# Biases by matmul, halves written across partitions, and a first convolution in half columns

## The chip, the cores and the metric

The kernel runs on one core of one Trainium2 chip. The core has five engines that work beside each other and wait for each other through semaphores: PE (TensorE: matrix products; its weight loads are listed apart as PEld), DVE (VectorE), ACT (ScalarE), POOL (GpSimd) and SP (SyncE, which here only issues DMA transfers). Data lie in SBUF, whose 128 partitions are the rows of every tile; PE writes its results to PSUM, from where ACT and DVE take them. The metric is the device time of one execution in microseconds (us), lower is better.

## What is computed

Four images of 128 channels and 64 by 64 = 4096 positions go through two layers. Layer 0 normalises the image, makes three 1x1 convolutions with a PReLU, and mixes the positions by a softmax over 4096 by 4096 scores. Layer 1 normalises each position's 128 channels, applies an attention with 16 heads of 8 channels whose queries, keys and values are all the same tensor, a feed-forward part, and at last a recurrence over the positions. The reference, cut to what matters here:

```python
def _L0_conv_ref(x, w1, b1, a1, w2, b2, a2, wa, ba, aa):
    e1 = _conv1x1(x, w1, b1, a1).reshape(N, -1, HW)      # 64 channels
    e2 = _conv1x1(x, w2, b2, a2).reshape(N, -1, HW)      # 64 channels
    asm = _conv1x1(x, wa, ba, aa).reshape(N, C, HW)      # 128 channels
    score = jnp.einsum('nci,ncj->nij', e1, e2)
    score = jax.nn.softmax(score, axis=2)
    out = jnp.einsum('nij,ncj->nci', score, asm)

def _L1_attn_ref(x, ...):
    qkv = _qz_ring(heads + rx_theta)
    attn = softmax(einsum('bhsd,bhtd->bhst', q, q) / np.sqrt(D))
    ctx = einsum('bhst,bhtd->bhsd', attn, q)
    attn_out = ctx @ w_comb.T + b_comb
    x1 = _ln(x + attn_out, g1, beta1)
    zf = jnp.cos(x1[..., :NQ_FFN]) * jnp.cos(ry_theta)
    h = jax.nn.relu(zf @ w1.T + b1)
    ffn_out = h @ w2.T + b2
    return _ln(x1 + ffn_out, g2, beta2)

def step(yt, wx_t):                                       # over all positions
    yt = jax.nn.sigmoid(wx_t + yt @ Vt)
```

## The kernel before

**Stages.** For each image n from 0 to 3 there is a convolution stage (`first_stage`, layer 0) and an attention stage (`second_stage`). The feed-forwards of image n run inside the convolution stage of image n+1, eight of them (one for 512 positions each), cut into small steps that are interleaved with that stage's own work; those of image 3 run alone in a `third_stage`. Then the recurrence runs and the output is written. In each stage the order of the instructions on PE, ACT and DVE (in attention on POOL too) is the order in which the code issues them, so an instruction that waits holds up all that stand behind it on its engine.

**Two float32 formats.** A float32 matmul is made of two passes over its columns. A float32r matmul is one pass and rounds its operands; where the kernel needs more precision it splits a number in a high part (rounded) and a low part (the rest) and stacks the two along the partitions, or makes two matmuls.

**The start of a convolution stage** (`layer0`). The image `xs` is normalised in eight pieces of 512 columns (`normalised`, L364, DVE). `both_convs(i)` convolves 1024 columns with w1 and w2 at once (L379, PE; result in PSUM pair `pc`), ACT makes the two halves of the PReLU (`y` L324, `z` L325), DVE joins them (L326) into `e1`, whose partitions 0 to 63 hold the first convolution and 64 to 127 the second. Then DVE writes the rounded second convolution to partitions 64 to 127 of `e2` (L386) and the rest to a scratch (L388), and two DMAs on SP's queue move 64 partitions each: `e1` low to `e1` high (L389), the scratch to `e2` low (L390). So `e2` has high and low parts of the second convolution stacked, and `e1` twice the first. `halves(ic)` splits 512 columns of `e1` into high and low parts (L425, L426) as the moving operand `hl`. `scores(ic, jp)` multiplies `e2` with both parts of `hl` (L442, two matmuls for each 128 rows), ACT takes the exponential (L446), DVE sums (L451, L454). `weigh` multiplies with `asmT` (L461), `take` copies the sum out (L473). `third_conv(i)` makes `asmT`: a matmul of ones with `ba_rows` writes the bias first (L396), then L405 adds the product; a PReLU follows. The order at the start is: pieces 0 and 1 normalised, `both_convs(0)` (the other six pieces within it, ahead of its L326), `halves(0)`, `third_conv(0)`, `both_convs(1)`, then the scores, with the other convolutions between them (list `pieces`, one popped at a time).

**Attention.** 8 head pairs by 4 query blocks. A block is a row of turns (20 in the first two blocks, 16 in the others); a turn makes scores for two key tiles and both heads (L956), exponentials (ACT, L968), and two turns later the product with the values (`weigh`, L807). Since scores are symmetric, a tile off the diagonal is used a second time, transposed: DVE transposes (L773), and after four turns of a group 16 `mirror_step`s (L786, eight small matmuls each) multiply into one of two halves of PSUM `misc`, and DVE adds that to `later` (L800), which frees the half. `finish` transposes the block's result (L841). How many mirror steps follow a turn is set by a credit: each turn adds a rate and each step takes one.

```python
rates = (3.3, 3.0) if b < NQB // 2 else (3.15, 3.0)
credit = min(credit + rates[0 if off else 1], 4.0)
```

A turn that is not `off` has its tiles on the diagonal; `end_of_all` is the last block of the last head pair. In that last block the statistics of the next image (L337 to L352) are issued too. What is left of the mirror steps after the last turn is done at the start of the next stage, around the first L364 and L379.

**A feed-forward** (`feed_forward`). POOL adds `bc_bc` (b_comb in every partition) to `x1` (L1075). PE transposes `q`, ACT copies it (`cT`, L1078), PE multiplies with `wc_sb` (L1083) and DVE adds `x1`, giving `v` (L1085). `v` is normalised (statistics on DVE, the power on POOL at L241, ACT at L283), DVE multiplies g1 (L1092), and POOL adds `fb2_bc` (which holds fb2 + beta1) into `x1` (L1093). A cosine of eight channels follows, then two matmul layers (L1129, ACT relu L1138, L1148 into `po`); L1158 adds `x1`, and two more normalisations and a residual (L1165, L1168) follow. In `third_stage` the last pieces of attention (`left`: L823 to L882) are done first, by DVE, POOL and ACT in turn.

**Setup.** Small weights are loaded on POOL's queue, then ACT's. `cos_steps` on `ry_sb` and a product with `f1_all` make `f_low`, part of which a DMA on SP (L311) moves to `f1_sb`.

Of the kernel before, what the change touches and what calls it, by code (L numbers as in the profile page):

```python
# [26 lines left out]
def kernel(  # L27
# [136 lines left out]
    ba_rows = const.tile([P, P], F32, tag="ba_rows", name="ba_rows")  # L164
    nc.gpsimd.memset(ba_rows, 0.0)
# [20 lines left out]
    wc_sb, bc_bc = load(w_combT, "wc_sb"), load_row(b_comb, "bc_bc")  # L186
# [9 lines left out]
    ba_all = setup_pool.tile([33, P], F32, tag="ba_all", name="ba_all")  # L196
    nc.gpsimd.memset(f1_all, 0.0)
    for i in range(2):
        nc.scalar.dma_start(out=ba_all[ds(32 * i, 1), :], in_=ba)
# [3 lines left out]
    fb1_sb, f2_sb, fb2_bc = load(fb1, "fb1_sb"), load(f2T, "f2_sb"), load_row(fb2, "fb2_bc")  # L203
# [8 lines left out]
    nc.vector.tensor_tensor(fb2_bc, fb2_bc, be1_bc, ALU.add)  # L212
# [80 lines left out]

    def blocks(ap):
        return ap.rearrange("p (k e) -> p k e", e=P)
# [8 lines left out]
    for _ in cos_steps(cry, ry_sb, ck, cr):  # L304
# [8 lines left out]
    nc.vector.tensor_copy(ba_rows[0:1, :].bitcast(F32R), ba_all[0:1, :])  # L313
    nc.vector.tensor_copy(ba_rows[32:33, :].bitcast(F32R), ba_all[32:33, :])
    nc.vector.tensor_tensor(
        ba_rows[32:33, :].bitcast(F32R), ba_all[32:33, :], ba_rows[32:33, :], ALU.subtract
# [38 lines left out]
    def layer0(n, xs, xh, norm, shifted, begin, meanwhile):  # L355
# [12 lines left out]
        e1, e2 = get("e", f"e1_{n}"), get("e", f"e2_{n}")  # L368
# [4 lines left out]

        def both_convs(i):

            cols = ts(i, 2 * IC)
            pc = pair_psum(f"pc{n}_{i}")
            for j in range(2):
                nc.tensor.matmul(  # L379
                    pc[:, j, :], w12_sb, xh[:, ts(2 * i + j, IC)], start=True, stop=True  # L380
                )
            y, z = mid_tile(f"y{n}_{i}"), mid_tile(f"z{n}_{i}")
            if i == 0:
                normalised(2, NIC)
            prelu(pair(e1[:, cols]), pc, y, z, (b12_sb, minus_b12), a12_sb)
            nc.vector.tensor_copy(pair(e2[CR:P, cols]).bitcast(F32R), pair(e1[CR:P, cols]))  # L386
            low = y[CR:P]
            nc.vector.tensor_tensor(low, pair(e1[CR:P, cols]), pair(e2[CR:P, cols]), ALU.subtract)  # L388
            nc.sync.dma_start(out=e1[CR:P, cols], in_=e1[0:CR, cols])  # L389
            nc.sync.dma_start(out=pair(e2[0:CR, cols]), in_=low)  # L390

        def third_conv(i):

            pc = pair_psum(f"pa{n}_{i}")
            for j in range(2):
                nc.tensor.matmul(  # L396
                    pc[:, j, :],
# [80 lines left out]
        if not shifted:  # L478
            halves(0)
# [1167 lines left out]
```

## Time and profile before

| what | us |
|---|---|
| three executions | 7203.8, 7194.3, 7195.15 (median 7195.15) |
| profiled execution, device time | 7196.66 |
| its span in the trace | 7194.9 |
| convolution stages (24 to 415, 1660 to 2165, 3420 to 3920, 5180 to 5690) | 391, 505, 500, 510 |
| attention stages (415 to 1660, 2165 to 3420, 3920 to 5180, 5690 to 6945) | 1245, 1255, 1260, 1255 |
| last feed-forwards (6945 to 7075) | 130 |
| recurrence and end (7075 to 7195) | 120 |

The stage borders are rounded to 5 us from the timeline; the convolution stage of image 0 is shorter since it has no feed-forwards in it. The engines over the span, from the first part of the page:

```profile
PE 6875.7 (96%) x92974; PEld 3726.6 (52%) x92974; DVE 5958.0 (83%) x8037; ACT 5994.8 (83%) x11903; POOL 2783.9 (39%) x9957
```

Each entry is an engine, its busy time, the share of the span, and its instructions. The costliest groups of the whole span (line, engine, operation, tiles and shapes, count; busy time and mean of one in ns; idle time of the engine just before, and what ended most of it):

```profile
L968 ACT ACTIVATE e<-s 128x1024 f32<-128x1024 f32 (+1 forms) x3480 | 2947.9, 888 | 89.6 <-PE s L956 40.7
L773 DVE STREAM_TRANSPOSE t<-e 128x1024 f32<-128x1024 f32 x2240 | 2586.2, 1209 | 10.1 <-ACT e L968 7.5
...
L786 PE MATMUL misc<-t,mirror 128*32 128x128 f32 x57344 | 1994.0, 273 | 28.4 <-DVE later L800 25.6
```

All three belong to attention. Busy time of PE overlaps from one matmul to the next, so it is read against the length of a stage, not summed.

### The profile page before, as it was taken

How to read it: one execution, taken by the hardware profiler on the slowest of the kernel's cores; microseconds unless marked ns; L12 is line 12 of the kernel's file. 1: busy time of each engine (PE TensorE's matmuls, PEld its weight loads, DVE VectorE, ACT ScalarE, POOL GpSimd, SP SyncE). 2: the span in 40 equal slices, each digit the busy share in tenths (PEclk: the TensorE clock that was granted, in tenths of full speed). 3: DMA queues.
4: the chain of work that ended last, by engine and by line, in shares of the span. 5: the costliest groups of instructions: out<-in, count | busy, mean ns of one | idle time of the engine just before them, and what ended most of it. 6: DMA issues, size and time to landing. Idle time of an engine off the chain costs nothing. (4 is left out here: it accounts for less than half of the span.)

```text
span 7194.9 us, 224876 instructions
## 1 busy us (share of the span) xinstructions
PE 6875.7 (96%) x92974; PEld 3726.6 (52%) x92974; DVE 5958.0 (83%) x8037; ACT 5994.8 (83%) x11903; POOL 2783.9 (39%) x9957
## 2 busy tenths in 40 slices
PE   8999999998989999999898999999999999999977
PEld 4545555555554555554555455555455555555546
DVE  6678899887778999889676998888877788898884
ACT  3479999995558999999455999999855699999976
POOL 0024444434223454443423354444432244444541
PEclk9999999999999999999999999999999999999988
DMA  1010000001111000000011100000001100000012
GB/s 39 30 40 26 29 20 22 21 8 38 39 40 44 25 21 20 21 23 21 29 40 43 37 22 21 21 24 22 23 30 39 45 33 21 22 26 27 11 59 108
DMA packets 85394, 221.20 MB, mean 31 GB/s; under 512 B 9490, under 2 KB 10644, under 8 KB 83588
## 3 DMA queue, kind: packets, MB, share of 16 engines
q1 hardware_dynamic: 79904, 195.10, 8.1%
q8 instruction: 731, 11.98, 0.7%
q10 hardware_dynamic: 4164, 11.41, 0.4%
q14 instruction: 307, 2.51, 0.1%
q0 software_dynamic: 288, 0.20, 0.0%
HBM read 141.63 MB, written 56.62 MB: 28 GB/s over the span
## 5 line engine op out<-in xcount | busy, mean ns | idle before, releaser
L968 ACT ACTIVATE e<-s 128x1024 f32<-128x1024 f32 (+1 forms) x3480 | 2947.9, 888 | 89.6 <-PE s L956 40.7
L773 DVE STREAM_TRANSPOSE t<-e 128x1024 f32<-128x1024 f32 x2240 | 2586.2, 1209 | 10.1 <-ACT e L968 7.5
L786 PEld LDWEIGHTS misc<-t,mirror 128*32 128x32 f32 x57344 | 1664.5, 110 | 1409.0 <-issue 1350.7
L786 PE MATMUL misc<-t,mirror 128*32 128x128 f32 x57344 | 1994.0, 273 | 28.4 <-DVE later L800 25.6
L968 ACT ACTIVATE xs<-s 128x1024 f32<-128x1024 f32 (+1 forms) x2152 | 1835.0, 893 | 33.7 <-PE s L956 19.9
L773 DVE STREAM_TRANSPOSE t<-xs 128x1024 f32<-128x1024 f32 x1344 | 1558.8, 1209 | 2.2 <-ACT xs L968 0.8
L807 PE MATMUL acc<-e,q_aug 128*32 128x512 f32 x11360 | 1524.5, 609 | 0.0
L956 PE MATMUL s<-queries,keys 32*128 32x512 f32 x9216 | 1228.6, 497 | 23.1 <-ACT e L968 16.7
L849 POOL COPY own<-o 32x36 f32<-32x36 f32 x2048 | 432.3, 211 | 1730.8 <-DVE o L841 1650.9
L461 PE MATMUL acc<-p,asmT 128*128 128x512 f32 x2048 | 960.9, 602 | 2.5 <-ACT taken L473 2.5
L807 PE MATMUL acc<-xs,q_aug 128*32 128x512 f32 x7072 | 942.2, 605 | 0.0
L446 ACT ACTIVATE p<-s 128x1024 f32<-128x1024 f32 x512 | 499.9, 1022 | 458.3 <-PE s L442 457.3
L454 DVE TENSOR_TENSOR total<-total,p 128x1024 f32<-128x1024 f32 x448 | 564.7, 1260 | 278.0 <-ACT p L446 255.0
L956 PEld LDWEIGHTS s<-queries,keys 32*128 32x128 f32 x9216 | 483.6, 182 | 517.7 <-issue 368.5
L874 POOL COPY other<-turned 32x64 f32<-32x64 f32 x1904 | 445.8, 234 | 640.6 <-DVE turned L864 562.1
L743 POOL COPY mirror<-q 32x128 f32<-32x128 f32 x2048 | 596.8, 291 | 239.3 <-PE misc L786 151.4
L968 ACT ACTIVATION_READ_ACCUMULATOR e<-s 128x1 f32 x2880 | 649.0, 225 | 0.0
L442 PE MATMUL s<-hl,e 128*128 128x512 f32 x2048 | 608.7, 440 | 29.5 <-DVE hl L426 22.8
L461 PEld LDWEIGHTS acc<-p,asmT 128*128 128x128 f32 x2048 | 383.2, 192 | 338.9 <-issue 314.0
L442 PEld LDWEIGHTS s<-hl,e 128*128 128x128 f32 x2048 | 393.2, 196 | 184.4 <-issue 98.9
L800 DVE TENSOR_TENSOR later<-later,misc 128x128 f32<-128x128 f32 (+1 forms) x576 | 162.6, 282 | 375.8 <-PE misc L786 372.6
L834 POOL COPY by_token<-by_key 32x4 f32<-32x4 f32 x2016 | 388.6, 193 | 85.1
(258 smaller groups left out, 4788.1 us busy)
## 6 DMA issues: line engine op xcount, KB each, us to landing
keys<-parts_dram SPq DMA_DIRECT2D x256, 256.0 KB
queries<-parts_dram SPq DMA_DIRECT2D x1024, 32.0 KB
fx<-x_dram SPq DMA_DIRECT2D x64, 256.0 KB
x_dram<-x SPq DMA_DIRECT2D x56, 256.0 KB
xs<-in_x_dram SPq DMA_DIRECT2D x16, 512.0 KB
t_dram<-t2T SPq DMA_DIRECT2D x32, 256.0 KB
t2s<-t_dram SPq DMA_DIRECT2D x16, 512.0 KB
parts_dram<-high SPq DMA_DIRECT2D x28, 256.0 KB
```

The source lines that it names most:

```text
L442: nc.tensor.matmul(s[:, j, :], stationary, moving, start=y == 0, stop=y == len(parts) - 1)
L446: nc.scalar.activation(p, s, AF.Exp)
L454: nc.vector.tensor_tensor(state[ic], state[ic], p, ALU.add)
L461: nc.tensor.matmul(state["acc", ic], asmT[:, ts(2 * jp + j, P)], p[:, j, :], start=jp == 0 and j == 0, stop=jp == NP - 1 and j == 1,)
L743: nc.gpsimd.tensor_copy(wv[ts(a, 32), s, :, :, ts(a, D)], own[ts(s, 32)])
L773: nc.vector.transpose(group["e"][h][:, k, :], es[h])
L786: nc.tensor.matmul(state["acc"][ts(2 * x + h, 32), :], state["w"][:, QT * (s // 4) + TG * x + s % 4, h, :], state["e"][h][:, :, ds(IC * x ...
L807: nc.tensor.matmul(it["in"]["acc"][ts(2 * h + x, 32), :], it["qa"][:, ds((2 * it["tiles"][x] + h) * V, 32)], it["e"][h][:, ts(x, IC)], sta ...
L849: nc.gpsimd.tensor_copy(own[ts(s, 32), ts(x, 4), h, :], ov[ts(2 * h + x, 32), s, :, 0:V])
L874: copy(to[ts(k, 32), h], tv[ts(2 * x + h, 32), k])
L956: nc.tensor.matmul(ss[h][:, x, :], keys[unit[x] // QT].bitcast(F32R)[r, ts(unit[x] % QT, P)], queries[b].bitcast(F32R)[r, :], start=True, ...
L968: nc.scalar.activation(es[h][:, ts(x, IC)] if split else es[h], ss[h][:, x, :] if split else ss[h].rearrange("p x c -> p (x c)"), AF.Exp, ...
```

## The change

1. *Biases of the feed-forward.* One tile `bias_rows` holds ba, b_comb and fb2 + beta1 as high part in partition 0 and low part in partition 32, zeros elsewhere. `bias_first` multiplies ones with one of the three and starts the accumulation; it serves the third convolution as before, and now also L1083 and L1148. The two POOL additions, and the tiles `bc_bc` and `fb2_bc`, go; `v` takes `x1`'s place, and `fhalf` has one buffer less.
2. *Parts of e.* One tile `e12` holds both convolutions; DVE writes the rounded second convolution to `e2` high, and the low part straight to `e2`'s partitions 0 to 63 (inputs in partitions 64 to 127). The DMAs L389 and L390 go. `halves` works on 64 partitions; its result is copied to the other 64 by a DMA on SP, or, for the first columns of each image, by two ACT copies.
3. *First pieces.* The first convolution's PReLU and joins go by half columns (512); the six later pieces are normalised in two lots behind the first joins; `third_conv(0)` uses two single PSUM tiles; `both_convs(1)` moves behind the first two scores, as the first of the popped pieces.
4. *Credit.* The cap goes from 4.0 to 4.75, and diagonal turns of the last block have a rate of 4.5. Mirror steps that follow the five turns of a group in the first two blocks become 4, 4, 3, 3, 2 (before 4, 3, 3, 3, 3); a group in the other blocks ends one turn earlier.

The diff, cut to its core:

```diff
-    ba_rows = const.tile([P, P], F32, tag="ba_rows", name="ba_rows")
+    bias_rows = const.tile([P, 3, P], F32, tag="bias_rows", name="bias_rows")
...
     for i in range(2):
-        nc.scalar.dma_start(out=ba_all[ds(32 * i, 1), :], in_=ba)
+        for k, ap in enumerate((ba, b_comb, fb2, be1)):
+            nc.scalar.dma_start(out=biases[ds(32 * i, 1), k, :], in_=ap)
...
-    nc.vector.tensor_copy(ba_rows[0:1, :].bitcast(F32R), ba_all[0:1, :])
-    nc.vector.tensor_copy(ba_rows[32:33, :].bitcast(F32R), ba_all[32:33, :])
+    for row in (0, 32):
+        at = slice(row, row + 1)
+        nc.vector.tensor_tensor(biases[at, 2], biases[at, 2], biases[at, 3], ALU.add)
+        nc.vector.tensor_copy(bias_rows[at].bitcast(F32R), biases[at, 0:3])
     nc.vector.tensor_tensor(
-        ba_rows[32:33, :].bitcast(F32R), ba_all[32:33, :], ba_rows[32:33, :], ALU.subtract
+        bias_rows[at].bitcast(F32R), biases[at, 0:3], bias_rows[at], ALU.subtract
     )
...
+    def bias_first(dst, k):
+        nc.tensor.matmul(
+            dst,
+            ones.bitcast(F32R),
+            bias_rows[:, k, :].bitcast(F32R).unsqueeze(1).broadcast_to([P, TG, P]),
+            start=True,
+            stop=False,
+            skip_group_check=True,
+        )
...
-        e1, e2 = get("e", f"e1_{n}"), get("e", f"e2_{n}")
+        e12, e2 = get("e", f"e12_{n}"), get("e", f"e2_{n}")
...
+        def conv_matmuls(i, js, to):
+            for j in js:
+                nc.tensor.matmul(
+                    to[:, j, :], w12_sb, xh[:, ts(2 * i + j, IC)], start=True, stop=True
+                )
+        def conv_relus(i, j0, j1, src):
+            y, z = mid_tile(f"y{n}_{i}_{j0}"), mid_tile(f"z{n}_{i}_{j0}")
+            nc.scalar.activation(y[:, j0:j1], src[:, j0:j1], AF.Relu, bias=b12_sb)
+            nc.scalar.activation(z[:, j0:j1], src[:, j0:j1], AF.Relu, bias=minus_b12, scale=-1.0)
+            return y, z
+        def conv_joins(i, j0, j1, y, z):
+            cols = slice((2 * i + j0) * IC, (2 * i + j1) * IC)
+            def parted(ap):
+                return ap.rearrange("p (a b) -> p a b", b=IC)
+            joined = parted(e12[:, cols])
+            nc.vector.scalar_tensor_tensor(
+                joined, z[:, j0:j1], a12_sb, y[:, j0:j1], ALU.mult, ALU.add
+            )
+            high, low = parted(e2[CR:P, cols]), parted(e2[0:CR, cols])
+            nc.vector.tensor_copy(high.bitcast(F32R), joined[CR:P])
+            nc.vector.tensor_tensor(low.bitcast(F32R), joined[CR:P], high, ALU.subtract)
         def both_convs(i):
-            cols = ts(i, 2 * IC)
             pc = pair_psum(f"pc{n}_{i}")
-            for j in range(2):
+            conv_matmuls(i, (0, 1), pc)
+            conv_joins(i, 0, 2, *conv_relus(i, 0, 2, pc))
+        def third_matmuls(i, j, to):
+            bias_first(to, 0)
+            for k in range(TG):
                 nc.tensor.matmul(
-                    pc[:, j, :], w12_sb, xh[:, ts(2 * i + j, IC)], start=True, stop=True
-                )
-            y, z = mid_tile(f"y{n}_{i}"), mid_tile(f"z{n}_{i}")
-            if i == 0:
-                normalised(2, NIC)
-            prelu(pair(e1[:, cols]), pc, y, z, (b12_sb, minus_b12), a12_sb)
-            nc.vector.tensor_copy(pair(e2[CR:P, cols]).bitcast(F32R), pair(e1[CR:P, cols]))
-            low = y[CR:P]
-            nc.vector.tensor_tensor(low, pair(e1[CR:P, cols]), pair(e2[CR:P, cols]), ALU.subtract)
-            nc.sync.dma_start(out=e1[CR:P, cols], in_=e1[0:CR, cols])
-            nc.sync.dma_start(out=pair(e2[0:CR, cols]), in_=low)
-        def third_conv(i):
-            pc = pair_psum(f"pa{n}_{i}")
-            for j in range(2):
-                nc.tensor.matmul(
-                    pc[:, j, :],
-                    ones.bitcast(F32R),
-                    ba_rows.bitcast(F32R).unsqueeze(1).broadcast_to([P, TG, P]),
-                    start=True,
-                    stop=False,
-                    skip_group_check=True,
-                )
-            for k in range(2 * TG):
-                nc.tensor.matmul(
-                    pc[:, k // TG, ts(k % TG, P)],
-                    xh[:, ts(2 * TG * i + k, P)],
+                    to[:, ts(k, P)],
+                    xh[:, ts(TG * (2 * i + j) + k, P)],
                     wa_sb,
                     start=False,
                     stop=True,
                     skip_group_check=True,
                 )
+        def third_conv(i):
+            pc = pair_psum(f"pa{n}_{i}")
+            for j in range(2):
+                third_matmuls(i, j, pc[:, j, :])
             to = pair(asmT[:, ts(i, 2 * IC)])
             if i % 2:
                 prelu_vector(to, pc, mid_tile(f"za{n}_{i}"), aa_sb)
             else:
                 prelu(to, pc, mid_tile(f"ya{n}_{i}"), mid_tile(f"za{n}_{i}"), (0.0, 0.0), aa_sb)
+        def first_pieces():
+            normalised(0, 1)
+            pc = pair_psum(f"pc{n}_0")
+            conv_matmuls(0, (0,), pc)
+            normalised(1, 2)
+            conv_matmuls(0, (1,), pc)
+            early = conv_relus(0, 0, 1, pc)
+            pas = [one_psum(f"pa{n}_0_{j}") for j in range(2)]
+            for j in range(2):
+                third_matmuls(0, j, pas[j])
+            conv_joins(0, 0, 1, *early)
+            if not shifted:
+                halves(0)
+            late = conv_relus(0, 1, 2, pc)
+            if not shifted:
+                for y in range(2):
+                    hl = state["halves", 0][:, y, :].bitcast(F32R)
+                    nc.scalar.copy(hl[CR:P], hl[0:CR])
+            def join_third(j):
+                ya, za = half_tile(f"ya{n}_0_{j}"), half_tile(f"za{n}_0_{j}")
+                prelu(asmT[:, ts(j, IC)], pas[j], ya, za, (0.0, 0.0), aa_sb)
+            join_third(0)
+            normalised(2, 4)
+            conv_joins(0, 1, 2, *late)
+            normalised(4, NIC)
+            return lambda: join_third(1)
         state = {}
         def halves(ic):
             hl = get("hl", f"hl{n}_{ic}")
-            src = e1[:, ts(ic, IC)]
-            nc.vector.tensor_copy(hl[:, 0, :].bitcast(F32R), src)
-            nc.vector.tensor_tensor(hl[:, 1, :].bitcast(F32R), src, hl[:, 0, :], ALU.subtract)
+            src = e12[0:CR, ts(ic, IC)]
+            high, low = hl[0:CR, 0, :], hl[0:CR, 1, :]
+            nc.vector.tensor_copy(high.bitcast(F32R), src)
+            nc.vector.tensor_tensor(low.bitcast(F32R), src, high, ALU.subtract)
+            if ic or shifted:
+                nc.sync.dma_start(out=hl[CR:P], in_=hl[0:CR])
             state["halves", ic] = hl
             if shifted:
                 state["less", ic] = row_max(n, ic, hl, e2)
...
-        normalised(0, 2)
-        both_convs(0)
-        if not shifted:
-            halves(0)
-        third_conv(0)
-        both_convs(1)
-        pieces = [lambda: third_conv(1)]
+        joins = first_pieces()
+        pieces = [lambda: (joins(), both_convs(1)), lambda: third_conv(1)]
...
                     rates = (3.3, 3.0) if b < NQB // 2 else (3.15, 3.0)
-                    credit = min(credit + rates[0 if off else 1], 4.0)
+                    if end_of_all and not off:
+                        rates = (0, 4.5)
+                    credit = min(credit + rates[0 if off else 1], 4.75)
...
-        nc.gpsimd.tensor_tensor(blocks(x1), blocks(x1), row4(bc_bc), ALU.add)
...
         pa = one_psum(f"pw{n}_{i}")
+        bias_first(pa, 1)
         for k in range(TG):
-            nc.tensor.matmul(pa[:, ts(k, P)], cT[:, ts(k, P)], wc_sb, start=True, stop=True)
-        v = get("fhalf", f"v{n}_{i}")
+            nc.tensor.matmul(
+                pa[:, ts(k, P)],
+                cT[:, ts(k, P)],
+                wc_sb,
+                start=False,
+                stop=True,
+                skip_group_check=True,
+            )
+        v = x1
         nc.vector.tensor_tensor(v, pa, x1, ALU.add)
...
-        nc.gpsimd.tensor_tensor(blocks(x1), blocks(v), row4(fb2_bc), ALU.add)
...
         po = one_psum(f"pf{n}_{i}")
+        bias_first(po, 2)
         for k in range(TG):
             for f in range(NF):
                 nc.tensor.matmul(
                     po[:, ts(k, P)],
                     hs[f // 2][:, f % 2, ts(k, P)],
                     f2_sb[:, f, :],
-                    start=f == 0,
+                    start=False,
                     stop=f == NF - 1,
+                    skip_group_check=True,
                 )
         yield
         u = im["q"][:, cols]
-        nc.vector.tensor_tensor(u, po, x1, ALU.add)
+        nc.vector.tensor_tensor(u, po, v, ALU.add)
```

More of the change, by code (lines that the diff above doesn't have):

```diff
@@ L162 @@
         nc.gpsimd.dma_start(out=a12_sb[ts(i, CR), :], in_=ap.partition_broadcast(CR))
-    ba_rows = const.tile([P, P], F32, tag="ba_rows", name="ba_rows")
-    nc.gpsimd.memset(ba_rows, 0.0)
+    bias_rows = const.tile([P, 3, P], F32, tag="bias_rows", name="bias_rows")
+    nc.gpsimd.memset(bias_rows, 0.0)
     for t in (a12_sb, aa_sb):
@@ L185 @@
     rx_bc = load_row(rx, "rx_bc")
-    wc_sb, bc_bc = load(w_combT, "wc_sb"), load_row(b_comb, "bc_bc")
+    wc_sb = load(w_combT, "wc_sb")
     f1_sb = const.tile([P, NF, P], F32, tag="f1_sb", name="f1_sb")
@@ L195 @@
     )
-    ba_all = setup_pool.tile([33, P], F32, tag="ba_all", name="ba_all")
+    biases = setup_pool.tile([33, 4, P], F32, tag="biases", name="biases")
     nc.gpsimd.memset(f1_all, 0.0)
     for i in range(2):
-        nc.scalar.dma_start(out=ba_all[ds(32 * i, 1), :], in_=ba)
+        for k, ap in enumerate((ba, b_comb, fb2, be1)):
+            nc.scalar.dma_start(out=biases[ds(32 * i, 1), k, :], in_=ap)
     for g in range(4):
@@ L202 @@
         nc.scalar.dma_start(out=ry_sb[ds(D * g, D), :], in_=ry)
-    fb1_sb, f2_sb, fb2_bc = load(fb1, "fb1_sb"), load(f2T, "f2_sb"), load_row(fb2, "fb2_bc")
+    fb1_sb, f2_sb = load(fb1, "fb1_sb"), load(f2T, "f2_sb")
     g1_bc, be1_z = load_row(g1, "g1_bc"), const.tile([P, D], F32, tag="be1_z", name="be1_z")
@@ L209 @@
     gamma_sb, beta_sb = load(gamma, "gamma_sb"), load(beta, "beta_sb")
-    nc.vector.tensor_tensor(fb2_bc, fb2_bc, be1_bc, ALU.add)
     nc.vector.tensor_copy(be1_z, be1_bc[:, 0:D])
@@ L1287, in first_stage @@
         n = im["n"]
-        ffn = dict(x1=(HALF, 3), fhalf=(HALF, 8), hT=(MID, 2))
+        ffn = dict(x1=(HALF, 3), fhalf=(HALF, 7), hT=(MID, 2))
         sums = dict(thalf=(HALF, 6), half=(HALF, 2), sums=(MID, 2), hl=(MID, 2))
```

## The prediction

> **What bounds the kernel now.** I read the table of windows by stage first, then what PE waits for inside the short stages, then the timeline around each wait. The first three columns are the stretch, its length, and PE busy.
>
> ```profile
> 415.00:1660.00 1245.00, 1233.88 (x21108) 624.40 (x21112) 1116.68 (x1202) 1212.93 (x2564) 530.72 (x2213) 0.99 0.07 24
> 1660.00:2165.00 505.00, 452.80 (x1960) 279.23 (x1953) 360.83 (x763) 270.83 (x362) 177.78 (x286) 0.96 0.12 37
> ...
> 6945.00:7075.00 130.00, 87.02 (x649) 73.67 (x642) 94.82 (x396) 78.12 (x186) 79.97 (x150) 0.74 0.26 94
> ```
>
> In attention (first line) PE is busy 1233.9 of 1245 us and ACT 1212.9: PE ends it, with ACT close behind. In a convolution stage PE is busy 452.8 of 505, so some 52 us are waits. In the last feed-forwards (third line) no engine is full (PE 87 of 130) and PE's mean clock is 0.74: a chain of waits. So time can be had where PE waits. What PE waits for at the start of image 1, and the timeline that leads to it (two lines of the table of waits: total, times, longest; then lines of the timeline: start, length, what, and in brackets the idle time before):
>
> ```profile
> PE s L442 <- DVE hl L426: 5.8, 1, 5.8
> PE misc L786 <- DVE later L800: 3.2, 1, 3.2
> ...
> 1660.39 4.77 DVE L364 TENSOR_SCALAR q<-xs,gm,r_g 128x512 f32<-128x512 f32 x4 [0.67 <-POOL r_g L241]
> ...
> 1666.46 3.70 PE L786 MATMUL misc<-t,mirror 128*32 128x128 f32 x128 [3.16 <-DVE later L800]
> ...
> 1671.26 1.11 ACT L324 ACTIVATE y<-pc,b_sb 128x1024 f32<-128x1024 f32 x1 [11.66 <-PE pc L379]
> ...
> 1676.81 0.52 SPq L389 DMA_DIRECT2D e<-e  x1
> ...
> 1679.97 0.43 DVE L425 CAST hl<-e 128x512 fp32r<-128x512 f32 x1 [3.30 <-DMA e<-e]
> ...
> 1681.23 3.75 PE L442 MATMUL s<-hl,e 128*128 128x512 f32 x8 [5.82 <-DVE hl L426]
> ```
>
> The reader is to see two stops in one chain. PE stands 3.16 us because L800 (which frees the accumulator) is queued on DVE behind four L364 that took 4.77 us; then 5.82 us, because the first scores need `hl`, `hl` needs both halves of `e1`, and these come by a DMA that DVE waits 3.30 us for. Images 2 and 3 show the same (5.83 and 3.15 for image 2); image 0 has only the second stop (5.24 at 38.58). After it eight L442 take 3.75 us; the eight at 1695.34 take 2.41. PE comes back cold. In the last feed-forwards (waits, then timeline):
>
> ```profile
> PE pw L1083 <- ACT cT L1078: 15.5, 8, 4.7
> PE pc L291 <- DVE q L882: 10.8, 1, 10.8
> ...
> 6956.76 4.92 POOL L1075 TENSOR_TENSOR fx<-fx,bc_bc 128x512 f32<-128x512 f32 x4
> 6956.86 5.46 DVE L874 COPY other<-turned 32x64 f32<-32x64 f32 x7
> ...
> 6963.47 1.59 DVE L874 COPY other<-turned 32x64 f32<-32x64 f32 x8
> ```
>
> Seven DVE copies take 5.46 us beside POOL's L1075 and eight take 1.59 after it; the 10.8 us wait for `q` (L882) hangs on them.
>
> **What the Trainium skill says.** "SBUF — State Buffer", Who interferes with whom: DVE copies, casts and tensor_scalars in a two-port mode and GpSimd instructions exclude each other for a whole instruction. The trace agrees: L364 takes 1.19 us (4.77/4) beside L1075 and 0.50 without it, L874 0.78 against 0.20. "TensorE: Matmul & The Clock Gate", What's actually happening: PE drops to half clock after some idle microseconds; the 3.75 us above agree. "DMA: Bandwidth & Descriptors", Anatomy of one DMA: about 2.0 us of fixed cost for a DMA of the GpSimd path; on SP's queue this trace shows 3.2 from issue to use, and I take that.
>
> **The change, part by part** (us; brackets are both bounds). The sum is made against the profiled execution, 7196.66, which is 1.5 above the median of 7195.15.
>
> *First piece, images 1 to 3.* Before, PE loses 3.16+5.82 = 9.0 in waits and (3.75−2.41) = 1.3 to the clock, 10.3 in all. After: L800 stands ahead of all L364 on DVE, and the 16 steps of the last group (16×0.215 = 3.4, 0.215 a step from L786) come before the first convolution, so the wait of 3.16 goes. PE then reaches the first half convolution at 1661.19+0.86+3.44 = 1665.5 (L786's start, 4 steps, 16 steps) and ends it 0.9 later. Half-column y and z take 2×0.63 (the 128x512 ACT rate) for 2×1.11; L326, L386, L388 on half the columns 0.65+0.36+0.62 for 1.28+0.69+1.22; L425 and L426 stay 1.07, the copy to the other partitions costs ACT 0.6; 3.30 for the DMA goes. First scores at 1666.4+1.3+1.6+1.1+0.6 = 1671.0, or 1669.6 with the earlier DVE start below; before 1681.23. That is 10.2 to 11.6 earlier, of which 1.7 are given back, since the convolution `pc_1` (4×0.43) is now after these scores. What is late next is ACT: the late relus and `join_third` stand beside the first exponentials, so I count −9.0 each, −27 [−33, −12]. The small end, −4 each, is the case where the order of work on DVE or ACT keeps more than half of the wait.
>
> *First piece, image 0.* No mirror steps fill PE. The chain loses 3.21 (DMA), 0.86 and 1.5 as above and gains the copy 0.6; first scores some 7 earlier, less 1.7 for `pc_1` and the time PE needs for the third convolution: −4.6 [−6, −3].
>
> *Start-up loads.* On ACT's queue four more issues net, about 0.4 each, stand ahead of `ry` and `f1`, from which `f_low` is made, whose DMA ends the 2.2 wait of the first L364. +1.4 [0, +2.5].
>
> *The other e DMAs and hl DMAs.* 32 transfers of 256 KB go, 28 of the same size come for `hl`, half a block of columns (over 20 us) ahead of use; DVE writes across partitions at the row of L388. Cost 0 where hidden; if the cover failed, 3.2 each. No sign of that: the lead is far over 3.2.
>
> *Credit.* The mirror steps per turn go from 4,3,3,3,3 to 4,4,3,3,2 for the first two query blocks; the total (1792 steps of 0.215 and 576 turns of 1.445 in an image) is the same. PE turns then take 1.445+0.215×(4, 4, 3, 3, 2) = 2.31, 2.31, 2.09, 2.09, 1.88 against ACT's 2.02 to 2.09, and three pairs of PSUM lie between them (over 1 us of lead). PE is the bound, so 0 [−8, +20].
>
> *Ends of attention.* On DVE one L337 of the next image (0.66) moves behind the last group's transposes, three times, −2; image 3's wait for ACT at 6936.10 (2.49) mostly goes, −2.3. Together −4.3 [−7, 0].
>
> *Starts of attention.* The first scores no longer wait for L589 (0.86 at 418.00); the transposes that follow start as before. −1 each, −4 [−9, 0].
>
> *Feed-forward biases beside convolutions.* 24×2 more matmuls of 128x512 float32r at 0.22 (spacing of L396) = +10.6 if all lie on the path; 48 POOL operations of about 1.38 (L1075, L1093) go, and their collisions with DVE. No chain ended in those POOL operations. +4 [−2, +10.6].
>
> *Third stage.* L874: 5.46 → 1.4 on the path to q, −4; L1075 twice ahead of `r_v` on POOL (2×1.26) and L1093's collisions (about 1.1 each, a few on the path) −6; plus 8 `po` biases ×0.22 in the stretch from 7018 to 7054 where L1148 (3.74 to 4.83 each) is back to back, +1.8. −8 [−12, −2].
>
> Sum: −27−4.6+1.4+0+0−4.3−4+4−8 = −42.5. From 7195.15 that is 7153.
>
> **Rivals.** (a) *The start is absorbed*: ACT takes over as soon as PE's wait goes (1213 of 1245 busy next door, two relus, two copies and a prelu before the first exponential), so only about 4 a stage remain: −16 for four stages, −4 for the third stage, rest 0: 7176. For: from its first exponential on ACT waits little (0.68 us before the one at 1685.02). Against: ACT idles 11.66 and 5.74 there. (b) *Slower*: two turns of 4 steps in a row use up what ACT has ahead, ACT idles, and ACT at 97% cannot make it up: 2×(2.31−2.09) = 0.44 for each of 256 pairs of such turns (4 images × 8 head pairs × 2 blocks × 4 groups), at most +112; it decides from 38% of that, for then +42 stands against −42. Counted at half (+56): 7153+56 = 7209. Against: PE, not ACT, is full in every attention window, and the lead of three PSUM pairs is longer than 0.44. (c) *More than summed*: with the POOL contention gone, DVE also runs the convolutions faster and the third stage loses 20 of its 43 idle us (130−87), 12 more than counted, and the convolutions another 16: 7153−28 = 7125. (d) *It doesn't do what it says*: the writes across partitions cost DVE double, 0.65 more for each of 16 low halves plus `hl`: +10 to +20 on DVE, which is not the bound there (361 of 505): inside the range.
>
> **How the numbers follow.** My forecast has 0.58 (7140 to 7168), (a) 0.18, (b) 0.11, (c) 0.13. About 0.2%, 14 us, is what a measurement of this kernel can tell from no change. Range for 8 in 10: 7127 (most of c) to 7182 (all of a). Faster: the forecast, (c), and nearly all of (a), less a little of each for the unknown of the credit: 0.81; same 0.09 (small ends of a and b); slower 0.10.
>
> **What would show it.** Right: no PE wait over 2 us for L426's successor and none for L800 at the starts of images 1 to 3; the stage windows of convolution some 8 us shorter each; the eight copies at L874's successor in some 1.6 us; attention windows within 5 us of 1245 to 1260. Wrong: attention windows longer by over 10 us with PE waiting for ACT's `e` or ACT for `s`; a wait for the `hl` DMA; the convolution's ACT waiting for PE no less than before.

## The result, and the profile after

| | median, us | lowest to highest | runs | ratio to the kernel before, 95% interval |
|---|---|---|---|---|
| kernel before | 7195.39 | 7193.87 to 7203.8 | 12 | |
| changed kernel | 7177.92 | 7173.96 to 7182.18 | 12 | 0.9975 [0.9966, 0.9983] |
| changed kernel, a second series beside other runs of the kernel before (7200.73) | 7173.66 | 7170.6 to 7175.35 | 5 | 0.9962 [0.9949, 0.9976] |

The change makes the kernel faster by 17.5 us in the first series and by 27.1 in the second, where 42 were forecast. The profiled execution of the changed kernel has a span of 7175.4 us, 19.5 less than before; this is what the ledger below adds up to. Three lines of the table of windows by stage; columns are the stretch, its length, then PE, PEld, DVE, ACT and POOL busy (with the number of instructions), PE's clock, and of DMA the share and GB/s:

```profile
408.00:1656.00 1248.00, 1235.86 (x21137) 625.05 (x21135) 1115.23 (x1204) 1206.77 (x2566) 532.63 (x2219) 1.00 0.07 24
1656.00:2166.00 510.00, 462.18 (x1974) 285.25 (x1974) 352.61 (x770) 275.12 (x372) 152.66 (x256) 0.97 0.12 37
...
6938.00:7055.00 117.00, 80.97 (x626) 69.59 (x618) 84.04 (x398) 76.99 (x184) 60.08 (x134) 0.84 0.28 103
```

Attention is as full as it was (PE 1235.9 of 1248), and the last feed-forwards fell from 130 to 117 us with PE's clock at 0.84 for 0.74. The second line can't be held against the 505 us of before: it ends 7.7 us after the last score of the stage, the line of before 0.7 us ahead of it. Measured between the same instructions, from attention's last product with the values to the last score, the convolution stages of images 1 to 3 took 505.0, 506.2 and 508.4 us before and 500.4, 501.8 and 501.8 after: 4.3 to 6.7 shorter, where some 8 were forecast. PE's waits around the start of image 1 in the changed kernel (total, times, longest; the first two lines from the end of attention, the others from the start of the convolutions):

```profile
PE misc L356 <- DVE gmv L353: 2.5, 1, 2.5
PE s L1011 <- ACT e L1023: 1.2, 1, 1.2
...
PE s L502 <- ACT hl L464: 2.4, 2, 2.2
PE s L502 <- ACT z L398: 1.3, 1, 1.3
PE s L502 <- ACT p L506: 1.1, 1, 1.1
```

L502 is the old L442. The waits of 5.8 us for `hl` and of 3.2 for `later` are gone, and so is the DMA on which the first hung. In their place stand a wait of 2.2 for ACT's copy of `hl` to the upper partitions and one of 1.3 for the PReLU of `pc_1`; and the wait for the statistics `gmv`, 1.27 before, is 2.55. One wait is quite new. It stands at the start of attention of images 1 and 3, here image 1:

```profile
PE acc L862 <- POOL q_aug L744: 5.5, 1, 5.5
PE misc L841 <- DVE later L855: 3.5, 1, 3.5
```

The new one is the first; the wait for `later` was there before, 4.7 us long.

**A ledger by landmarks.** Both kernels make the same scores and products in the same number, so the start of the n-th one can be compared between the two traces. A lag is the start in the changed kernel minus that in the kernel before; negative is earlier. For each image: the 1st, 65th and last of the 512 score matmuls of the convolutions (L442, L502 after); the attention's products with the values (L807, L862 after) when 1/16 and 15/16 of them are done, and the last one.

| image (us) | score 1 | score 65 | score 512 | product 1/16 | product 15/16 | last product |
|---|---|---|---|---|---|---|
| 0 | −6.1 | −3.5 | −4.7 | −3.8 | −1.6 | −2.8 |
| 1 | −12.8 | −9.0 | −7.4 | −3.6 | −1.4 | +0.3 |
| 2 | −9.7 | −5.6 | −4.1 | −7.7 | −5.6 | −4.0 |
| 3 | −15.3 | −11.7 | −10.7 | −6.8 | −4.4 | −7.9 |

At the end the lag is −19.5. The steps between columns, summed over the images, stand against the steps of the prediction. "Again" is a second profiled execution of the same changed kernel, from the second series; what differs between the two columns does not come from the change. (Steps may be 0.1 off by rounding.)

| step of the prediction | forecast | measured | again | between which landmarks |
|---|---|---|---|---|
| start-up loads | +1.4 | −0.6 | +0.7 | up to the first convolution |
| first piece, image 0 | −4.6 | −4.1 | −3.2 | to its score 512 |
| first piece, images 1 to 3 | −27 | −19.8 (−6.2, −5.9, −7.7) | −22.2 | last product to score 65 |
| biases beside the convolutions | +4 | +4.1 | +4.8 | score 65 to 512 |
| starts of attention | −4 | +5.0 (+0.9, +3.8, −3.6, +3.9) | +4.8 | score 512 to 1/16 |
| credit | 0 | +8.9 (2.1 to 2.4 an image) | +10.7 | 1/16 to 15/16 |
| ends of attention | −4.3 | −1.4 (−1.2, +1.7, +1.6, −3.5) | −7.4 | 15/16 to the last product |
| third stage | −8 | −11.7 | −11.8 | to the end of the span |
| sum | −42.5 | −19.6 | −23.5 | |

### The profile page after: what moved, and what is told of

The parts are those of the page before. It is cut to its first block, busy times and chain, and to the rows that moved or that the text cites. A ratio compares the mean times of both kernels' runs of the same rounds, so it can differ in the third digit from the quotient of the medians.

```text
span 7175.4 us, 224965 instructions
## 1 busy us (share of the span) xinstructions
PE 6874.2 (96%) x93038; PEld 3724.9 (52%) x93038; DVE 5912.0 (82%) x8054; ACT 5974.8 (83%) x11927; POOL 2707.9 (38%) x9893
## 5 line engine op out<-in xcount | busy, mean ns | idle before, releaser
L828 DVE STREAM_TRANSPOSE t<-e 128x1024 f32<-128x1024 f32 x2240 | 2587.2, 1208 | 10.3 <-ACT e L1023 7.7
L841 PE MATMUL misc<-t,mirror 128*32 128x128 f32 x57344 | 1982.4, 273 | 21.3 <-DVE later L855 17.5
L862 PE MATMUL acc<-e,q_aug 128*32 128x512 f32 x11360 | 1528.5, 610 | 11.2 <-POOL q_aug L744 11.0
L862 PE MATMUL acc<-xs,q_aug 128*32 128x512 f32 x7072 | 942.2, 605 | 0.0
L1023 ACT ACTIVATION_READ_ACCUMULATOR e<-s 128x1 f32 x2880 | 692.1, 240 | 0.0
L502 PE MATMUL s<-hl,e 128*128 128x512 f32 x2048 | 609.3, 440 | 19.8 <-ACT hl L464 9.4
L502 PEld LDWEIGHTS s<-hl,e 128*128 128x128 f32 x2048 | 391.7, 196 | 174.9 <-issue 72.3
```

The costliest lines, as they stand in the source:

```text
L502: nc.tensor.matmul(s[:, j, :], stationary, moving, start=y == 0, stop=y == len(parts) - 1)
L828: nc.vector.transpose(group["e"][h][:, k, :], es[h])
L841: nc.tensor.matmul(state["acc"][ts(2 * x + h, 32), :], state["w"][:, QT * (s // 4) + TG * x + s % 4, h, :], state["e"][h][:, :, ds(IC * x ...
L862: nc.tensor.matmul(it["in"]["acc"][ts(2 * h + x, 32), :], it["qa"][:, ds((2 * it["tiles"][x] + h) * V, 32)], it["e"][h][:, ts(x, IC)], sta ...
L1023: nc.scalar.activation(es[h][:, ts(x, IC)] if split else es[h], ss[h][:, x, :] if split else ss[h].rearrange("p x c -> p (x c)"), AF.Exp, ...
```

## The experiments

Ten more kernels ran, one of them twice, and the changed kernel once more. Ratios are to the kernel before on the same chip in the same series; differences in us between kernels of different series are taken from the landmarks.

### One buffer: `fhalf` at 8 again

```diff
-        ffn = dict(x1=(HALF, 3), fhalf=(HALF, 7), hT=(MID, 2))
+        ffn = dict(x1=(HALF, 3), fhalf=(HALF, 8), hT=(MID, 2))
```

> The changed kernel with fhalf at 8 buffers again, so that the tiles of the convolution stage lie where they lay before. Theory (placement): in images 1 and 3 the memset of mirror on POOL waits for PE's last transpose of taken, because one buffer less has moved the attention's tiles onto taken; with 8 buffers both waits of PE for q_aug (5.51 us each) go, and the time falls by 7 to 11 us, to 7167 to 7171. Rival (POOL is late of itself): the waits of 5.5 us stay, 7178. Second rival (something else is late there, such as the wait for later): the q_aug waits go, but the first products with the values come hardly earlier, 7175 to 7178.

Measured: 7165.16 us, ratio 0.9951 [0.9934, 0.9968]. The second time, in a series with the changed kernel itself:

> The changed kernel with fhalf at 8 once more. Theory (placement): 9 to 12 less than the run beside it, ratio to the kernel before 0.995 to 0.9965. Rival (the first comparison took its 12 from a lucky clock at the image ends): the same ratio as the changed kernel, within 0.0007.

> The changed kernel once more, on the same chip as the next run. Theory (the half clock after the 2.55 us wait for gmv at the ends of images 1 and 2 is not tied to the kernel): another execution shows it at other image ends or at none, and the last products with the values move by some 3 us at each such end. Rival (it is tied to the order of work): the same two ends show it again. Time near 0.9975 of the kernel before.

Measured: 0.9954 [0.9940, 0.9967] with 8 buffers, 0.9962 [0.9949, 0.9976] with 7; medians 7166.89 and 7173.66. The ratio stayed where the first run had it and within 0.0008 of the kernel beside it; the two intervals overlap, so the ratios alone do not settle it. But the two kernels ran side by side, and their five times each do not overlap (7164.89 to 7169.17 with 8 buffers, 7170.6 to 7175.35 with 7); the gain is 6.8 us, less than the 9 to 12 of the theory. The traces show where it stands. In the timeline of POOL before the attention of image 1, the kernel before has

```profile
2157.36 1.81 POOL L677 MEMSET mirror<- 128x2048 f32 x1 [10.73 <-DMA parts_dram<-low]
2159.11 6.94 POOL L689 COPY q_aug<-q 32x112 f32<-32x112 f32 x16
```

the changed kernel

```profile
2168.95 1.81 POOL L732 MEMSET mirror<- 128x2048 f32 x1 [17.75 <-PE pt L291]
2170.70 5.02 POOL L744 COPY q_aug<-q 32x112 f32<-32x112 f32 x16
```

and the changed kernel with 8 buffers

```profile
2150.93 1.81 POOL L732 MEMSET mirror<- 128x2048 f32 x1 [9.09 <-DVE total L514]
2152.68 6.94 POOL L744 COPY q_aug<-q 32x112 f32<-32x112 f32 x16
```

The memset clears a tile of the attention stage. With 7 buffers it is released by the last transposes that PE makes in the convolution stage (`pt`, of the tile `taken`), so POOL starts 12 us later than before, and the copies of `q_aug` behind the memset arrive when PE has long been waiting. That the tile then lies on the memory of `taken` is inferred from this releaser; the trace shows no addresses. With 8 buffers no wait for `q_aug` is left in any image. (Why image 2 is spared, where the memset starts at 3913.59 with 7 buffers for 3916.12 before, is not shown.) Between the two executions of the last series the lag falls by 4.7 at the first product of image 1 and by 4.7 at that of image 3; 1.2 of each come back in a longer wait for `later` (4.6 for 3.5), so that 3.5 an image remain. With 1.2 of chance ahead of them, the span is 8.3 shorter. The step "starts of attention" of the ledger is −1.8 and −2.5 in the two profiles with 8 buffers, for +5.0 and +4.8. What the second expectation asks of the half clock is answered under "Ends of attention" below: the second execution shows it at none of the ends.

### Part 1 alone: biases by matmul

The kernel before with the bias matmuls, without the two POOL additions, and with `v` in `x1`'s place; then the same with 7 buffers.

```diff
-        nc.gpsimd.tensor_tensor(blocks(x1), blocks(x1), row4(bc_bc), ALU.add)
...
+        bias_first(pa, 1)
...
-        v = get("fhalf", f"v{n}_{i}")
+        v = x1
...
-        nc.gpsimd.tensor_tensor(blocks(x1), blocks(v), row4(fb2_bc), ALU.add)
...
+        bias_first(po, 2)
```

> The kernel before with part 1 of the change alone (biases of the feed-forwards by matmul, no POOL additions, v in x1's place; fhalf still 8). Theory: +3.5 us in each of three convolution stages (+10.5), and the last feed-forwards some 10 us shorter, because the 10.8 us wait for q and those for cT hang on DVE copies that stand beside POOL's L1075; in sum about 7195, no change. Rival (the last feed-forwards gained from the shorter end of attention, not from POOL): they stay at about the length before, and the time is 7205.

Measured: 7178.04, ratio 0.9970 [0.9958, 0.9983]; the span of the profile is 19.0 under that of the kernel before. Both theories had it at no gain or a loss, and both fell in the sum; the last feed-forwards give 10.3, as the first expected. So part 1 alone, with 8 buffers, is as fast as the whole change with 7 (0.9975 and 0.9962), as far as these intervals tell. The rest comes from the starts of images 1 to 3, which gain 2.0, 4.7 and 5.8 from the last product to score 65 (timeline of this kernel; L377 is the old L364, L792 the old L786):

```profile
1659.49 1.92 DVE L377 TENSOR_SCALAR q<-xs,gm,r_g 128x512 f32<-128x512 f32 x4 [0.67 <-POOL r_g L241]
...
1662.71 3.70 PE L792 MATMUL misc<-t,mirror 128*32 128x128 f32 x128 [0.30 <-DVE later L806]
```

The four normalisations take 1.92 us without POOL beside them, for 4.77, and the wait for `later` behind them is 0.30, for 3.16. Nothing in DVE's order was changed here. The wait is 2.9 us shorter in each image; the rest of these gains was not taken apart. And the 48 matmuls, with POOL's 48 additions gone in exchange, cost little: the lag from score 65 to the last moves by −0.8, +1.0 and +0.9 in the three stages.

> Part 1 alone as in the earlier run, now with fhalf at 7 buffers as in the changed kernel. Theory (placement): PE waits for q_aug, 4 to 6 us, appear at the start of attention of images 1 and 3, and the time rises by 8 to 10 over part 1 with 8 buffers, to 7186 to 7188. Rival (the wait needs the other parts of the change as well, the earlier end of the convolutions): no such waits, 7178.

Measured: 7188.65, ratio 0.9983 [0.9976, 0.9990]; 9.5 more in the span than with 8 buffers, of which 6.8 stand at the starts of attention of images 1 and 3. PE's waits at the start of the attention of image 1 show the wait for `q_aug` without any other part of the change:

```profile
PE acc L813 <- POOL q_aug L695: 5.5, 1, 5.5
```

So the buffer count makes it without the other parts, and half of what part 1 brings is lost by it (12 us under the kernel before, for 23).

### The bias matmuls twice, and not at all

```diff
-        bias_first(pa, 1)
+        for _ in range(1 if final else 2):
+            bias_first(pa, 1)
```

(and so for `po`; `fhalf` at 8)

> fhalf at 8, and every bias matmul of the feed-forwards inside the convolution stages made twice (48 float32r matmuls of 128x512 more; the second begins the sum anew, so the numbers stay). Theory (the matmuls fall into PE's waits for the feed-forwards' vector steps): the lag against the run with 8 buffers grows by less than 1 us a stage, under 3 in all. Rival (each costs PE its 0.22, which the forecast took as the upper bound): +3.5 a stage, +10.6 in all.

Measured: 7174.52, ratio 0.9964 [0.9952, 0.9977]. From score 65 to the last, the lag against the run with 8 buffers grows by 2.2 us in each stage, 6.5 for 48 matmuls, or 0.14 for each 0.22 of PE work: between the two theories. The first 48 cost 4.8 with 8 buffers, but POOL's additions went in exchange, so the two figures are not a like pair. The profiled execution is the slowest of the six; the rest of the 13 us by which it is longer stands mostly at the ends of images 0 and 2 (3.0 and 4.5), where PE came back from the wait for `gmv` or just after at half clock.

```diff
+        if not final:
+            nc.gpsimd.tensor_tensor(blocks(x1), blocks(x1), row4(bc_bc), ALU.add)
...
+        if final:
+            row_first(pa, bc_bc)
```

> fhalf at 8 as in the run before, and the feed-forwards inside convolution stages take their biases by POOL as before the change (no bias matmul there); the last feed-forwards have both biases by PE, as float32 products of ident with the rows (0.43 us each for 0.22). Theory (PE pays the biases in full): from the first to the last score of images 1 to 3 the changed kernel lost 5.4, 5.7 and 4.6 us; 3.5 a stage come back, so 10 less than the run with 8 buffers: 7157 to 7161. Rival (POOL's additions cost DVE as much as the matmuls cost PE): no difference to the run with 8 buffers, 7167 to 7171.

Measured: 7182.2, ratio 0.9974 [0.9966, 0.9983], so slower than with the matmuls, not faster: both theories missed. From score 65 to the last the lag moves by +2.4, +0.3 and +1.2 in the three stages, with the matmuls (8 buffers) by +1.6, +1.8 and +1.4: PE got back 0.8 of 10.6. In exchange 5.1 us are lost in the last feed-forwards, where the two bias products were float32 in this run (the trace has two records of 0.43 us for each, 0.86 together, and one of 0.22 for each float32r product; the expectation counted half), and 6.9 at the start of image 2. There DVE's sum `v` (the old L1085) waits for POOL, which is still at attention's copies, and with it `asmT` and PE:

```profile
3476.36 0.69 DVE L1159 TENSOR_TENSOR v<-pw,fx 128x512 f32<-128x512 f32 x1 [4.71 <-POOL own L938]
```

In the kernel before, DVE came to this sum some 10 us later (3481.81, for 3471.65 when this wait began) and found POOL done. So without part 1 the earlier first piece runs into POOL's work.

### Part 4: the credit

```diff
-                    credit = min(credit + rates[0 if off else 1], 4.75)
+                    credit = min(credit + rates[0 if off else 1], 4.75 if end_of_all else 4.0)
```

> The changed kernel with the cap of the credit at 4.0, except in the last block of the last head pair, where it stays 4.75. Theory (uneven turns): the changed kernel loses 0.31 us a head pair against the kernel before, in turns of 0 and 2 mirror steps in which PE runs into the wait for ACT; with the old cap the 2.2 us per image come back and the time falls by 9, to 7169. Rival (the loss has another source, such as the clock or the transfers): the lag curve in attention still falls by 0.3 a pair, 7178. The end of each image should stay as it is in the changed kernel, since its last block keeps the cap.

Measured: 7174.05, ratio 0.9964 [0.9951, 0.9976]. The lag inside attention is flat, as the theory had it (−3.0 to −2.9 in image 0, −9.7 and −9.7 in image 2); the changed kernel loses 0.3 for each head pair, evenly. But the 9 us of the theory do not show in the time, which is that of the changed kernel in its second series (0.9962). With 8 buffers as well:

> The changed kernel with both corrections: fhalf at 8 buffers, and the cap of 4.75 only in the last block of the last head pair. Theory (the two losses are independent): 12 less than the changed kernel for the placement and 9 for the credit, about 7156, with a flat lag curve inside attention and no PE wait for q_aug. Rival (they share a wait at the start of attention): only the larger of the two comes back, 7165.

Measured: 7165.55, ratio 0.9952 [0.9936, 0.9969], the same as with 8 buffers alone. That is the rival's number, but not its reason: the waits for `q_aug` are gone and the lag is flat again, where with 8 buffers alone it loses 2.5 to 2.8 us an image, but from 15/16 to the last product this kernel loses 0.3 to 1.2 an image, where the one with cap 4.75 throughout gains 1.2 to 3.4. So the higher cap loses 2 to 3 us per image in the middle, and about as much comes back in the last half head pair. Part 4 alone, on the kernel before:

```diff
-                    credit = min(credit + rates[0 if off else 1], 4.0)
+                    if end_of_all and not off:
+                        rates = (0, 4.5)
+                    credit = min(credit + rates[0 if off else 1], 4.75)
```

> The kernel before with part 4 alone (cap 4.75, rate 4.5 for the diagonal turns of the last block). Theory: 2.2 us lost in each of four attentions (+9), and at the end of images 0 to 2 the wait of 3.16 for later shrinks, since the last group but one is done before the normalisation starts (-3 each): about no change, 7193 to 7197. Rival (the shorter wait only moves PE's stop to the scores that wait for hl): +9, 7204.

Measured: 7190.44, ratio 0.9986 [0.9979, 0.9993], a little under what the theory had and far from the rival. Its wait for `later` at the starts of images 1 to 3 is under 0.9 us, and that for ACT's `e` 1.22 for 2.65, while the one for `gmv` is 2.55 for 1.27. Inside attention the lag grows by 2.7 to 2.9 an image.

### Parts 2 and 3 alone

The kernel before with `e12`, `conv_joins`, `halves` on 64 partitions and `first_pieces`; biases by POOL, credit and buffers as before. Its edit is the diff above without those parts.

> The kernel before with parts 2 and 3 alone (e across partitions, first pieces in half columns); biases of the feed-forwards on POOL, credit and fhalf as before. Theory (the 3.16 us wait for later belongs to POOL's L1075 beside the four L364, and is shared by parts 1 and 3): 4 less for image 0 and 4 to 7 less for each of images 1 to 3 once 64 score matmuls are done, so 16 to 25 in all, 7170 to 7179. Rival (the first scores come earlier but all that was put behind them takes the gain back): under 8 in all, over 7187.

Measured: 7187.92, ratio 0.9983 [0.9975, 0.9990]. That is 12.9 us under the kernel before of its series, between the two theories. From the last product to score 65 it gains 4.9 in image 1 and 7.8 in image 3, with a wait for `later` under 0.9; in image 2 it loses 0.4. There DVE's `v` waits 5.00 us for POOL as in the run with POOL's biases, PE waits 3.91 for `asmT` behind it and comes back at half clock, and 6.7 are lost between scores 49 and 57. (The profiled execution is the third slowest of 18, and shows 3.6 of the 12.9 us; how much of this loss the others had is not known.)

### The statistics two turns earlier

```diff
-                    if end_of_all and (at == 0 or at >= len(tiles) - NIC - 2):
+                    if end_of_all and (at == 0 or at >= len(tiles) - NIC - 4):
```

(`fhalf` at 8)

> fhalf at 8, and the statistics of the next image (L350) issued two turns earlier in the last block, so that DVE has one of them less behind the last transposes. Theory (the 2.55 us wait for gmv stands on DVE's order): it falls below 1.3 and the last transposes come no later, 1 us less at each of three ends, 2 to 4 in all. Rival (DVE is full there and ends at the same time whatever the order): the wait moves to the scores or the mirror steps, no difference.

Measured: 7181.84, ratio 0.9979 [0.9970, 0.9987], a miss: the wait for `gmv` rose to 5.73, 5.73 and 4.11 us at the three image ends. The edit moves the statistics' matmul forward on PE by two turns, but DVE delivers only 2.0 us earlier (`gmv` at 1652.61 for 1654.61 at the end of image 0); PE stops earlier in its own order.

## Why the prediction was right or wrong

**Where the missing 23 us stand.** Of −42.5 the profiled execution brought −19.6. The starts of attention are worse than forecast by 9.0 us, the credit by 8.9, the first piece of images 1 to 3 by 7.2 and the ends of attention by 2.9; the third stage and the loads are better by 5.7. In the second execution the ends are better than forecast and the credit is worse.

**The sign and most steps held.** The 5.8 and 3.2 us waits are gone. Image 0 (−4.1 for −4.6), the biases beside the convolutions (+4.1 for +4) and the third stage (−11.7, inside [−12, −2]) came as worked out. In the last feed-forwards the copies that stood beside L1075 now take

```profile
6946.82 1.60 DVE L929 COPY other<-turned 32x64 f32<-32x64 f32 x8
6949.58 1.59 DVE L929 COPY other<-turned 32x64 f32<-32x64 f32 x8
```

and the wait for `q` fell from 10.8 to 7.2.

**The step that failed is "Starts of attention", −4 [−9, 0].** It looked at PE, ACT and DVE alone, and measured +5.0, outside its bounds. The part of the change that decides it, `fhalf` from 8 buffers to 7, was told in the change and costed nowhere: with 7 buffers POOL's memset at the stage border waits for PE's last transposes, and the count of buffers alone brings this wait in and takes it away. The price is 5.5 us of waiting, 3.5 net, in two of four images; with 8 buffers the step is −1.8, inside its bounds.

**"First piece, images 1 to 3", −27, was 7 too high.** The first scores came 10.0, 10.0 and 11.3 earlier, about the 10.2 to 11.6 that was worked out. But 3.6 to 4.1 of it were given back by score 65, not 1.7: besides `pc_1` there is the new wait of 1.3 for its PReLU. ACT is late next, as the text said, but sooner than it was priced.

**The cause of the 3.16 us was told by half, and is shared.** The text put it down to DVE's order and counted it under part 3. The order matters: parts 2 and 3 alone bring L800's successor ahead of most normalisations and leave 0.84. But so does POOL's L1075 beside the four L364: part 1 alone, with DVE's order as it was, takes the wait from 3.16 to 0.30; and part 4 alone leaves 0.7 or less. So it was there to be won once, 9.5 us for three images. From the last product to score 65 of images 1 to 3 the three parts alone gain 12.5, 12.3 and 11.7 us, 36.4 together; the whole change gains 19.8, and 22.2 in its second execution. So 14 to 17 us of these gains are shared; the wait counted three times would make 19. The times say less: the three ratios 0.9970, 0.9983 and 0.9986 make 0.61% together, 44 us, where the whole change brings 33 to 35 with 8 buffers and 18 to 27 with 7, and each interval is 5 to 9 us wide to either side. The page of the Trainium skill that the prediction cites, "SBUF — State Buffer", Who interferes with whom, tells of just this collision, in which a DVE instruction in a two-port mode and a GpSimd instruction keep each other out, and the 1.92 against 4.77 us of part 1 alone agrees with it; the step did not use it.

**The credit's 0 [−8, +20] was +8.9 in the middle of attention,** inside its bounds, and near 0 with what comes back at the image ends. The step looked at the first two query blocks; the trace has the loss in the other two. A group there ends one turn earlier, which leaves a turn without any mirror step, where the kernel before had one with one step. Here such a turn begins at 2431.15, and the next at 2432.58:

```profile
2431.15 0.51 PE L1011 MATMUL s<-queries,keys 32*128 32x512 f32 x4
...
2432.58 0.77 PE L1011 MATMUL s<-queries,keys 32*128 32x512 f32 x4
2432.61 0.19 ACT L1023 ACTIVATION_READ_ACCUMULATOR xs<-s 128x1 f32 x1
```

The empty turn takes PE 1.43 us and ACT about 2.0, so PE has caught up with ACT: of the four score matmuls of the next turn (0.77 us for 0.51) the last two start 0.05 us after an instruction of ACT ends, and so they do in all 12 such turns of the six middle head pairs of image 1. These 12 take 2.575 us each, for 2.355 of the 12 in the same place before: 2.6 us, where the six head pairs as a whole are 1.9 longer. With the cap at 4.0 they take 2.356 again. The table of waits does not list this, since PE's matmul records overlap: its gaps there sum to 0.6 us in both kernels.

**What became of the rivals.** The time is close to that of (a), 7176 (its sum makes 7175), but not for its reason: the first pieces brought 24 us where it left 16, the third stage 11.7 where it left 4, and 18 were lost in steps that it put at nothing. That the number fits is luck. (b) had the sign of the middle, but not the mechanism: turns of four steps that follow another of four, its case, take 2.308 us in the six middle head pairs, as the prediction had them, and there are 30 of them, not 48. (d) fell: the write across partitions (L414) takes 1.22 us for 64x1024, as L388 did.

**Ends of attention, −4.3, brought −1.4, and −7.4 the second time.** PE's wait for ACT fell from 2.5 or 2.6 to 1.22 at the ends of images 0 to 2 (to 0.4 at that of image 3), but there the wait for `gmv` took as much. And the clock has a part that is chance. In the profiled execution PE comes back from this wait at the end of image 1 like this:

```profile
3414.05 0.59 PE L356 MATMUL misc<-gmv,grp 128*128 128x1 f32 x2 [2.56 <-DVE gmv L353]
...
3418.59 3.65 PE L862 MATMUL acc<-e,q_aug 128*32 128x512 f32 x16
```

and in the second profiled execution of the very same kernel like this:

```profile
3417.19 0.38 PE L356 MATMUL misc<-gmv,grp 128*128 128x1 f32 x2 [2.56 <-DVE gmv L353]
...
3419.95 1.93 PE L862 MATMUL acc<-e,q_aug 128*32 128x512 f32 x16
```

The wait is the same and the 16 products take 3.65 or 1.93 us; the granted clock is 0.50 from 3414 to 3422 us in the first and 1.00 from 3417 to 3422 in the second. The second lost nothing at the ends of images 1 and 2, where the first lost 3.0 us each, and its span is 4.0 shorter.

## What to carry to other kernels

Count the buffers of a stage as part of its timing: one buffer less can move the tiles that the next stage puts on the same memory, and the engine that clears or fills one may then wait for a reader it never had to do with; the queue to look at is that of the engine that starts the next stage. When work is shifted between turns, look at the turns that are left with none as well as at those that get more. Before a wait is credited to one part of a change, ask which other parts would remove it too: what several of them remove is paid once. And compare two kernels by the same instruction at many places, not by stage lengths: a loss of 0.3 us a head pair and a gain at the end of each image cancel in every total. The second execution of the same kernel tells how much of such a loss is chance.

## What the runs showed of the hardware

A wait of 2.55 us left PE at half clock (0.50) at two image ends in one execution and at full clock in the next, of the same kernel, so a single profile may carry some 3 us of chance at each such wait. DVE's 128x512 tensor_scalar takes 0.48 us alone (1.92/4) and 1.19 beside POOL's addition of 128x512. Float32r matmuls of 0.22 us put into a stage where PE has waits, 48 of them for 48 additions taken from POOL, cost 0.02 to 0.09 us each (1.2 us in part 1 alone, 4.1 in the whole change); 48 more, with nothing taken away, cost 0.14 each. A DVE tensor_tensor that reads 64 partitions and writes the other 64 took as long as one that does not cross (1.22 us for 64x1024).
